# Loads in parts, input stages one at a time, and four attention ticks drawn into the last retention turn

## The chip, the cores and the metric

The kernel runs on one core of one Trainium2 chip. Its engines are TensorE (PE in the profile, with its weight loads as PEld), VectorE (DVE), ScalarE (ACT), GpSimd (POOL) and SyncE (SP), each with its own queue of instructions, worked off in order. The metric is the time of one execution on the device in microseconds (us), lower is better, given as a median of several runs.

## The reference

Two post-norm layers on `x` of shape (2, 1024, 128), all in float32:

```python
x = layernorm(x + retention(x))        # 8 heads of key width 64, value width 128: q, k rotated, decay mask,
                                       # group norm per head, gate silu(x Wg), output Wo
x = layernorm(x + mla_then_moe(x))     # x + mla(rmsnorm(x)): 16 heads of 8, keys and values from a latent
                                       # of 64, rotary, causal softmax; then x + moe(rmsnorm(x)), 4 experts,
                                       # hidden 512, each token goes through its best expert
x = layernorm(x + attention(x))        # 16 heads of 8, biases on q, k, v, softmax over all 1024 keys
                                       # (two corner scores set to -1e9)
x = layernorm(x + x @ ternary(weight)) # weight rounded to -1, 0, 1 times its mean size
```

## The kernel before

The 2048 tokens are two sequences (`b`) of 1024. Work goes by chunks of 128 tokens in the first part and by blocks of 512 tokens (`k` = 0, 1 in each sequence) in all later ones. Both parts are written inside `tc.manual_schedule()`: what the program emits first runs first on its engine.

**Retention turns.** A loop over `n_chunks` = 16 chunks holds one *turn* per chunk. Turn `n` finishes chunk `n - 1` and prepares the ones after it, in this order: `scores(n)` (PE `psc`, DVE `sm`, PE `pout` with the carried state), `keys_by_token` (PE `pk`, DVE `kd`), `sines(n + 1)` (POOL multiplies `swap` by the sine table), `rotated(n + 1)` (DVE adds `swap` into `qk`, POOL makes `qd`), `gated(n - 1)` and `affine` (PE `pt`, ACT `og`), `weighted` (PE `pout`), `carry` (PE `pst`, POOL `old`, DVE `state`), the DVE product `og * sg`, `group_norm(n)` (ACT `sq`, DVE `ss`, POOL `rstd`), `rotary(n + 2)` (PE `pr`, ACT `plain`, and four DMAs on SP's queue that copy `plain` into `swap` with its halves exchanged), `cosines(n + 2)`, `gate(n + 1)` (PE `pg`), `layer_norm` of a block that is complete, `aside(n, 0)`, `normal(n)` (DVE `on`), `output(n - 1)` (PE `py` with `r_wo`, DVE residual and statistics), `values(n + 1)` (PE `pv`), `aside(n, 1)` and `transpose_x(n + 3)` (PE `xT_ps`). `swap` for chunk 2, called swap(2) below, is thus issued in turn 0 and read by POOL at the start of turn 1.

**Late loads.** `load_late()` runs once ahead of turn 0 and issues 28 DMAs on SP: the rest of the rotary table `r_cs`, `r_wo`, then 13 weight slices, then 4 broadcasts of `mcs`, 8 small bias loads and `rowb`.

**Work drawn into the turns.** `aside(n, where)` looks up `plan[(n, where)]` and advances a generator by so many stages. The generators are `pad` (`padding(0)`: POOL clears `qT`, `v_aug`; ACT sets `kT`) and `ins[k]` (`mla_inputs(0, k, True)`), which makes queries, keys and values of block `k` of sequence 0. Its stages are `sq`; `ss`, `rstd`, `xn`; `xn_ps`, `xnT`; `pl`, `plat`; `stats` with the rotated queries (PE `mpr` twice, DVE `mrope` twice, DVE `dense`, four DMAs of `spread`); `apply`; `lat_ps`, `latT`; `mpv` with the rotated keys (again `mpr`, `mrope`, `dense`, `spread`). It needs block `k` after its `layer_norm`: block 0 is ready from turn 5 on, block 1 from turn 9.

**Banks.** The turns use PSUM pools `rps` (two buffers of two banks: `rwide`), `rpo` (two banks: `rbank`) and `racc` (two banks: `pout`). After the loop `rp.close()` frees all of them, and `ring_of` hands out eight banks in turn to all later work; the ring's pool waits for everything that used the freed memory. SBUF pools `late`, `work` and `jobs` likewise lie on memory that retention used.

**Attention ticks.** `chain_tick(t)` issues, for four heads, the scores of item `t` with their row maxima on DVE (`sc`, `spare` or `parts`), the transposed scores of item `t - AHEAD` with the exponentials on ACT (`sct`, `es`; `AHEAD` = 11), a causal cut on POOL (`bar`), and the products of item `t - 12` (PE `acc`, ACT `part`, POOL `oT`). Ticks 0 to 15 serve sequence 0, block 0; a step is 4 ticks there and 8 in block 1. `side_work(t)` runs ahead of tick `t` from tick 3 on and advances two lanes of `Job`s in order of their lists: the light lane is `padding(1)`, `setup()` (loads 2 MB of expert weights, makes the ternary weight), `mla_inputs(1, 0)`, `mla_inputs(1, 1)` and later ones; the heavy lane's experts begin at tick 30. A job not yet due at its tick holds up those behind it in its lane; a stage that yields 0 is followed by the next stage in the same tick.

After turn 15 the program before emits: `gated(15)`, `affine`, tick 0, the product `og * sg`, the last stage of `ins[1]`, tick 1, `output(15)`, tick 2, `layer_norm`, and then ticks 3 onwards with side work.

Of the kernel before, what the change touches and what calls it, by code (L numbers as in the profile page):

```python
# [14 lines left out]
P = 128  # L15
# [45 lines left out]
def block_kernel(  # L61
# [96 lines left out]
    def slot(name):  # L158
        return banks[0](name)

    def ring_of(pool):
        turn = [0]

        def bank(name):

            turn[0] += 1
            return pool.tile([P, BT], F32, tag=f"b{turn[0] % 8}", name=name)

        return bank

# [79 lines left out]
    def mla_inputs(b, k, alone=False):  # L250
        got = {}
        yield from rmsnorm_T(x1[b][k], col("norm1"), got)
        xnT = got["xnT"]

        def rotary_dense(dst, w, ws, src, tag):
            tt = scratch("mrope", "mrope", (P, 2, BT))
            table = mcs.rearrange("p (a t) -> p a t", a=2)[:, :, block_of(k)]
            for i, name in enumerate((w, ws)):
                pr = slot("mpr")
                mm(pr, name, src)  # L260
                if alone:
                    nc.vector.tensor_tensor(tt[:, i, :], pr, table[:, i, :], ALU.mult)
# [6 lines left out]
            engine.tensor_tensor(dense, tt[:, 0, :], tt[:, 1, :], ALU.add)  # L269
            spread(dst, k, dense)  # L270

        pl = by_tile(xnT, mw["wdkv"], "pl")
        plat = scratch("plat", "plat", (P, NC, 64))
        nc.scalar.copy(flat(plat), pl[:, : NC * 64])
        yield 1
        mv, r = stats(tiles(plat))
        rotary_dense(qT[b], mw["wq"], mw["wqs"], xnT, "sq")
        yield 2
        apply(tiles(plat), tiles(plat), mv, r)
        yield 1  # L280
        tp = slot("lat_ps")
# [3 lines left out]
        nc.scalar.activation(  # L285
            latT, tp[:64, :], AF.Identity, bias=col("ln_b", 0, 64), scale=col("ln_g", 0, 64)
        )
        yield 1
        pv = by_tile(latT, mk["wuv"], "mpv")
        nc.scalar.copy(  # L290
            v_heads(b)[:, k * NC : (k + 1) * NC, :, :HD],
            pv.rearrange("p (c h d) -> p c h d", c=NC, d=HD),
        )
        rotary_dense(kT[b], mk["wuk"], mk["wuks"], latT, "xn")
        yield 1

# [179 lines left out]


    with ExitStack() as rc:
        rp = ExitStack()
        rps = rp.enter_context(tc.tile_pool(name="rps", bufs=2, space=PSUM))  # L480
        rpo = rp.enter_context(tc.tile_pool(name="rpo", bufs=2, space=PSUM))
        racc = rp.enter_context(tc.tile_pool(name="racc", bufs=1, space=PSUM))
        rconst = rc.enter_context(tc.tile_pool(name="rconst", bufs=1))
        two = rc.enter_context(tc.tile_pool(name="r2", bufs=2))

# [31 lines left out]
        pads, padded = qT[0].rearrange("p g t -> p (g t)"), [0]  # L517

        def load_late():
            nc.sync.dma_start(out=cs[:, :, 2 * P :], in_=cs_in[:, :, 2 * P :])  # L520
            load_w("wo", nc.sync)
            for got, src, pack, n_rows, prefix in (
                (mw, m_w, M_W, P, "m"), (mk, m_k, M_K, 64, "mk"), (lw, l_w, L_W, P, "l")
            ):
                for name, (at, n) in pack.items():
                    if name not in ("w1", "w2"):
                        if n == NH * HW:
                            got[name] = pads[:n_rows, padded[0] : padded[0] + n]
                            padded[0] += n
                        else:  # L530
                            got[name] = const.tile([n_rows, n], F32, name=f"{prefix}_{name}")
                        nc.sync.dma_start(out=got[name], in_=src[:, at : at + n])
            for j in range(GH):
                nc.sync.dma_start(
                    out=mcs[dense_rows(j), :],
# [8 lines left out]
            nc.sync.dma_start(out=rowb, in_=rows.partition_broadcast(P))  # L544

        def dense_weights():

# [239 lines left out]
        def layer_norm(m, r):  # L787
# [22 lines left out]
        with tc.manual_schedule():  # L810
# [11 lines left out]
            for n in range(n_chunks):  # L822
                nxt, before = n + 1 < n_chunks, n > 0
# [4 lines left out]
                if nxt:  # L828
                    sines(n + 1)
                    rotated(n + 1)  # L830
# [11 lines left out]
                if nxt:  # L842
                    gate(n + 1)
                if block:
                    layer_norm(*block)
                    block = None
# [1 line left out]
                normal(n, r)  # L848
                if before:
                    block = output(n - 1, og)  # L850
                if nxt:
                    values(n + 1)
                aside(n, 1)
                if n + 3 < n_chunks:
                    transpose_x(n + 3)
                if n == 2:
                    dense_weights()

        rp.close()
# [36 lines left out]
    pools["work"] = ctx.enter_context(tc.tile_pool(name="work", bufs=2))  # L896
    jobs_sb = scratch_of[0] = ctx.enter_context(tc.tile_pool(name="jobs", bufs=1))

    def project(src, w, name, got, tag):

# [158 lines left out]
    class Job:  # L1059
# [179 lines left out]
```

## Time and profile before

| what | value |
|---|---|
| median of 3 runs | 1206.19 us (1205.71 to 1208.68) |
| the profiled execution's own time | 1211.32 us |
| its span, first to last instruction | 1209.6 us |
| mean granted clock of TensorE | 0.962 |
| busy: PE, PEld, DVE, ACT, POOL | 1112.6, 608.0, 830.1, 711.2, 479.0 us |
| start of turns 0, 1, 2 (first `psc`) | 21.4, 33.3, 54.8 us |
| start of turn 15 | 245.8 us |
| start of tick 4 on DVE, of tick 12 on DVE | 285.0, 308.8 us |

All durations below are from this one profiled execution, whose time is 5.1 us above the median. A busy share over the whole span mixes the retention turns (to about 280 us) with the attention ticks; a part of the change is read in the stretch where it lies. In a timeline line the first two numbers are start and duration, x is the count of instructions merged into it, and the bracket is the idle time of the engine before it with what ended that wait.

### The profile page before, as it was taken

To read this page: it belongs to the slowest core of one execution; us is meant where nothing else is said; L and a number is where in the kernel's file an instruction comes from. 1 tells how busy PE (TensorE), PEld (TensorE's weight loads), DVE (VectorE), ACT (ScalarE), POOL (GpSimd) and SP (SyncE) were. 2 spreads that over 40 slices of the span, in tenths; PEclk is the share of its full clock that TensorE was granted. 3 is DMA by queue.
4 is the path that set the end of the run, shared out by engine and by line. 5 is a ranking of instruction groups with operands and counts; after the bars stand their busy time and mean duration, and the time that the engine had idled before them with its cause. 6 is when DMAs were issued, how large, how long until landed. Compare 5 with 4: busy or idle time off the path is not lost.

```text
span 1209.6 us, 22194 instructions
## 1 busy us (share of the span) xinstructions
PE 1112.6 (92%) x8554; PEld 608.0 (50%) x8554; DVE 830.1 (69%) x1822; ACT 711.2 (59%) x1439; POOL 479.0 (40%) x491
## 2 busy tenths in 40 slices
PE   6899999988989999999999999999989989998993
PEld 5688778855444545455544454444433333333321
DVE  3467677657666666776666668667788878888822
ACT  2355544431656555654565547556768877886892
POOL 4365544513544433443434334333233333333342
PEclk9899999975889999999999999999999999999996
DMA  8211112102000000010000001000100000000000
GB/s 256 72 37 45 40 41 44 36 9 80 19 10 10 1 1 2 4 20 1 1 15 6 2 3 19 2 1 1 19 10 2 2 1 10 1 2 9 2 1 9
DMA packets 14841, 25.57 MB, mean 21 GB/s; under 512 B 2960, under 2 KB 8400, under 8 KB 14352
## 3 DMA queue, kind: packets, MB, share of 16 engines
q1 hardware_dynamic: 14080, 22.30, 7.6%
q8 instruction: 67, 1.10, 0.4%
q0 software_dynamic: 224, 1.05, 0.2%
q10 hardware_dynamic: 432, 0.81, 0.2%
q14 instruction: 38, 0.31, 0.1%
HBM read 10.13 MB, written 1.05 MB: 9 GB/s over the span
## 4 chain that ended last, share of the span: by engine, by line
PE 72%; DVE 15%; POOL 5%; issue 3%; ACT 2%; DMA 1%; SPq 0%; POOLq 0%; DVEq 0%; ACTq 0%
PE sc L82 16%; PE acc L82 15%; PE sct L82 12%; PE pmoe L82 5%; PE ph L82 5%; DVE parts L350 4%; DVE spare L345 2%; PE py L82 2%; PE pv L82 2%; PE pr L82 2%; PE pout L707 1%; PE pg L82 1%; ACT es L394 1%; PE o_ps L186 1%; PE psc L82 1%
## 5 line engine op out<-in xcount | busy, mean ns | idle before, releaser
L394 ACT ACTIVATE es<-sct 128x512 f32<-128x512 f32 (+3 forms) x896 | 427.4, 560 | 213.4 <-PE sct L82 160.9
L350 DVE TENSOR_REDUCE parts<-sc 128x1 f32<-128x512 f32 x640 | 397.4, 683 | 94.5 <-PE sct L82 67.0
L82 PE MATMUL sc<-kT,qT 32*128 32x512 f32 (+3 forms) x1792 | 427.1, 587 | 0.9 <-DVE parts L345 0.9
L82 PE MATMUL sct<-qT,kT 32*128 32x512 f32 (+3 forms) x1792 | 411.7, 577 | 1.4 <-DMA qT<-m_rows 1.1
L420 POOL TENSOR_TENSOR oT<-oT,part 128x512 f32<-128x512 f32 (+3 forms) x192 | 217.1, 1131 | 399.0 <-ACT part L419 395.0
L82 PE MATMUL acc<-es,v_aug 128*32 128x512 f32 (+3 forms) x1792 | 222.8, 561 | 40.0 <-DVE parts L350 28.4
L82 PEld LDWEIGHTS sc<-kT,qT 32*128 32x128 f32 x1792 | 169.9, 190 | 141.1 <-DVE parts L350 74.3
L82 PEld LDWEIGHTS sct<-qT,kT 32*128 32x128 f32 x1792 | 179.2, 184 | 45.0 <-issue 22.4
L345 DVE CUSTOM_DVE_ANT_0 spare<-sc,causal 128x512 f32<-128x512 f32 (+3 forms) x256 | 125.6, 490 | 55.5 <-PE sc L82 21.3
L82 PEld LDWEIGHTS acc<-es,v_aug 128*32 128x32 f32 x1792 | 37.9, 108 | 197.1 <-DVE parts L350 112.5
L419 ACT COPY part<-acc 128x512 f32<-128x512 f32 (+3 forms) x192 | 105.9, 552 | 42.6 <-PE acc L82 33.0
L402 POOL TENSOR_SCALAR_AFFINE_SELECT es<-es 128x512 f32<-128x512 f32 x64 | 40.6, 635 | 101.6 <-ACT es L394 101.6
L764 ACT ACTIVATE og<-pt,cols_sb 128x128 f32<-128x128 f32 x128 | 46.3, 467 | 37.5 <-PE pt L756 37.5
L82 PEld LDWEIGHTS pmoe<-m_w,hT 128*128 128x128 f32 x512 | 59.6, 192 | 15.9 <-DVE parts L350 8.8
L82 PE MATMUL pmoe<-m_w,hT 128*128 128x128 f32 x512 | 65.0, 280 | 0.4
L82 PE MATMUL ph<-xnT,m_w 128*128 128x512 f32 x128 | 62.4, 610 | 0.0
L118 POOL TENSOR_TENSOR rstd<-rstd,nhalf 128x4 f32<-128x4 f32 (+1 forms) x44 | 54.6, 1242 | 3.6
L638 POOL TENSOR_TENSOR swap<-swap,r_cs 128x1024 f32<-128x1024 f32 x16 | 38.7, 2419 | 26.4 <-DMA swap<-plain 26.4
L943 DVE TENSOR_SCALAR hT<-ph,cols_sb 128x512 f32<-128x512 f32 x32 | 24.0, 751 | 34.5 <-PE ph L82 34.5
L82 PE MATMUL py<-r_wo,og 128*128 128x128 f32 x256 | 37.0, 305 | 11.2 <-issue 5.4
L955 DVE SCALAR_TENSOR_TENSOR moe_acc<-pmoe,oh,moe_acc 128x128 f32<-128x128 f32 x64 | 22.5, 351 | 35.2 <-PE pmoe L82 34.8
L661 ACT COPY v<-pv 128x1024 f32<-128x1024 f32 x16 | 16.2, 1012 | 51.6 <-PE pv L82 51.6
(177 smaller groups left out, 1198.6 us busy)
## 6 DMA issues: line engine op xcount, KB each, us to landing
swap<-plain SPq DMA_DIRECT2D x64, 128.0 KB
qT<-dense SPq DMA_DIRECT2D x32, 64.0 KB
kT<-dense SPq DMA_DIRECT2D x32, 64.0 KB
m_w<-in_m_w SPq DMA_DIRECT2D x2, 1024.0 KB
x<-in_x SPq DMA_DIRECT2D x4, 256.0 KB
mcs<-in_m_const SPq DMA_DIRECT2D x4, 256.0 KB
out<-ob SPq DMA_DIRECT2D x4, 256.0 KB
r_rest<-in_r_const POOLq DMA_DIRECT2D x1, 774.0 KB, 7.9
```

The lines of the kernel that those rows point to most:

```text
L82: nc.tensor.matmul(o, lhsT, rhs, start=start, stop=stop)
L118: nc.gpsimd.tensor_tensor(r, r, nhalf[:, :n], ALU.pow)
L345: nc.vector.tensor_tensor_reduce(out=spare[:, :n], in0=sc[:, :n], in1=causal[:, BT - n :], scale=1.0, scalar=-3.0e38, op0=ALU.add, op1=ALU ...
L350: nc.vector.tensor_reduce(part, sc[:, :n], AX.X, ALU.max)
L394: nc.scalar.activation(es[n_item][:, j, :n], sct[:, :n], AF.Exp, scale=scale)
L402: nc.gpsimd.affine_select(out=d, in_=d, pattern=[[0, GH], [1, P]], compare_op=ALU.is_ge, fill=0.0, base=0, channel_multiplier=-1,)
L419: nc.scalar.copy(part[:, lo:], acc[:, lo:])
L420: nc.gpsimd.tensor_tensor(sums[i][:, lo:], sums[i][:, lo:], part[:, lo:], ALU.add)
L638: nc.gpsimd.tensor_tensor(swap[n], swap[n], table(n, 1), ALU.mult)
L764: nc.scalar.activation(og[:, a, g, :], pt[a][:, g, :], AF.Identity, bias=col("gn_b", h), scale=col("gn_w", h))
L943: nc.vector.tensor_scalar(hT[:, f, :], ph, bias, 0.0, ALU.add, ALU.max)
L955: nc.vector.scalar_tensor_tensor(acc[:, c, :], py[:, :P], oh[:, c, e : e + 1], acc[:, c, :], ALU.mult, ALU.add)
```

## The change

`load_late` becomes a generator in three parts: `r_cs` and `r_wo` are issued ahead of turn 0 as before; the 13 weight slices after `rotary(2)` in turn 0; the 13 DMAs of `mcs`, biases and `rowb` after `rotary(3)` in turn 1. `mla_inputs` gets two more places to pause, and `plan` now takes nearly every place once, one stage at a time, from (5, 1) on; block 1's stages all lie in turns 11 to 15. The last turn is written out by itself: its PSUM accumulators `racc` get a pool on the other side that closes only after `normal(15)`, the ring gets six banks first and two later, ticks 0 to 3 are placed among the last chunk's steps, and the ring and the SBUF pools `late`, `work`, `jobs` wait tile by tile. `setup()` may start from tick 12 only.

```diff
-    def ring_of(pool):
+    def ring_of(pools):
...
+            at = turn[0] % 8
             turn[0] += 1
-            return pool.tile([P, BT], F32, tag=f"b{turn[0] % 8}", name=name)
+            return pools[at // 6].tile([P, BT], F32, tag=f"b{at}", name=name)
...
         mv, r = stats(tiles(plat))
+        yield 0
         rotary_dense(qT[b], mw["wq"], mw["wqs"], xnT, "sq")
...
+        yield 0
         rotary_dense(kT[b], mk["wuk"], mk["wuks"], latT, "xn")
...
-        rp = ExitStack()
+        rs, rp = ExitStack(), ExitStack()
+        racc = rs.enter_context(tc.tile_pool(name="racc", bufs=1, space=PSUM, side="right"))
...
-        racc = rp.enter_context(tc.tile_pool(name="racc", bufs=1, space=PSUM))
...
             load_w("wo", nc.sync)
+            yield
...
                         nc.sync.dma_start(out=got[name], in_=src[:, at : at + n])
+            yield
...
             nc.sync.dma_start(out=rowb, in_=rows.partition_broadcast(P))
+            yield
...
-            (3, 1): (pad, 1), (4, 1): (pad, 1), (5, 1): (pad, 1), (6, 1): (pad, 3),
-            (7, 0): (ins[0], 2), (7, 1): (ins[0], 1), (8, 0): (ins[0], 1), (8, 1): (ins[0], 1),
-            (9, 0): (ins[0], 1), (9, 1): (ins[0], 1), (10, 0): (ins[0], 2),
-            (12, 0): (ins[1], 2), (13, 1): (ins[1], 1), (14, 0): (ins[1], 1),
-            (15, 0): (ins[1], 1), (15, 1): (ins[1], 2), (16, 0): (ins[1], 2),
+            (3, 1): (pad, 1), (4, 0): (pad, 1), (4, 1): (pad, 1), (5, 0): (pad, 3),
+            (5, 1): (ins[0], 1), (6, 0): (ins[0], 1), (7, 0): (ins[0], 1), (7, 1): (ins[0], 1),
+            (8, 0): (ins[0], 1), (8, 1): (ins[0], 1), (9, 0): (ins[0], 1), (9, 1): (ins[0], 1),
+            (10, 0): (ins[0], 1), (10, 1): (ins[0], 2),
+            (11, 0): (ins[1], 1), (11, 1): (ins[1], 1), (12, 0): (ins[1], 1), (12, 1): (ins[1], 1),
+            (13, 0): (ins[1], 1), (13, 1): (ins[1], 1), (14, 0): (ins[1], 1), (14, 1): (ins[1], 1),
+            (15, 0): (ins[1], 1), (15, 1): (ins[1], 2),
...
-            load_late()
+            late_loads = load_late()
+            next(late_loads)
...
+                next(late_loads, None)
+                gate(n + 1)
...
+            n = n_chunks - 1
+            sm = scores(n)
+            pt, og = gated(n - 1)
+            affine(n - 1, pt, og, range(RH))
+            weighted(n, sm)
+            nc.vector.tensor_tensor(og, og, sg[n - 1], ALU.mult)
+            r = group_norm(n)
+            aside(n, 0)
+            output(n - 1, og)
...
-        banks[0] = ring_of(ctx.enter_context(tc.tile_pool(name="ring", bufs=1, space=PSUM)))
-
+        ring.append(ctx.enter_context(
+            tc.tile_pool(name="ring", bufs=1, space=PSUM, reuse_waits="tile")
+        ))
+        banks[0] = ring_of(ring)
         with tc.manual_schedule():
-            n = n_chunks - 1
+            chain_tick(0)
+            normal(n, r)
+            rs.close()
+            ring.append(ctx.enter_context(tc.tile_pool(
+                name="ring2", bufs=1, space=PSUM, side="right", reuse_waits="tile"
+            )))
+            aside(n, 1)
+            chain_tick(1)
             pt, og = gated(n)
             affine(n, pt, og, range(RH))
-            chain_tick(0)
+            chain_tick(2)
             nc.vector.tensor_tensor(og, og, sg[n], ALU.mult)
-            aside(n_chunks, 0)
-            chain_tick(1)
             block = output(n, og)
-            chain_tick(2)
+            chain_tick(3)
             layer_norm(*block)
...
-    late = ctx.enter_context(tc.tile_pool(name="late", bufs=1))
+    late = ctx.enter_context(tc.tile_pool(name="late", bufs=1, reuse_waits="tile"))
...
-        Job(0, ends(0, 0, 0), setup()),
+        Job(12, ends(0, 0, 0), setup()),
...
-        for tick in range(3, last_tick):
+        for tick in range(4, last_tick):
```

More of the change, by code (lines that the diff above doesn't have):

```diff
@@ L819, in block_kernel @@
             rotated(0)
-            load_late()
+            late_loads = load_late()
+            next(late_loads)
             block = None
-            for n in range(n_chunks):
-                nxt, before = n + 1 < n_chunks, n > 0
+            for n in range(n_chunks - 1):
+                before = n > 0
                 keeps = not opens(n + 1)
@@ L827, in block_kernel @@
                     kd = keys_by_token(n)
-                if nxt:
-                    sines(n + 1)
-                    rotated(n + 1)
+                sines(n + 1)
+                rotated(n + 1)
                 if before:
@@ L841, in block_kernel @@
                     cosines(n + 2, rotary(n + 2))
-                if nxt:
-                    gate(n + 1)
+                next(late_loads, None)
+                gate(n + 1)
                 if block:
@@ L850, in block_kernel @@
                     block = output(n - 1, og)
-                if nxt:
-                    values(n + 1)
+                values(n + 1)
                 aside(n, 1)
@@ L857, in block_kernel @@
                     dense_weights()
+            n = n_chunks - 1
[7 more added lines that the diff above has]
+            output(n - 1, og)
+        ring = []
         rp.close()
-        banks[0] = ring_of(ctx.enter_context(tc.tile_pool(name="ring", bufs=1, space=PSUM)))
+        ring.append(ctx.enter_context(
+            tc.tile_pool(name="ring", bufs=1, space=PSUM, reuse_waits="tile")
+        ))
+        banks[0] = ring_of(ring)
         with tc.manual_schedule():
-            n = n_chunks - 1
+            chain_tick(0)
[6 more added lines that the diff above has]
+            chain_tick(1)
             pt, og = gated(n)
             affine(n, pt, og, range(RH))
-            chain_tick(0)
+            chain_tick(2)
             nc.vector.tensor_tensor(og, og, sg[n], ALU.mult)
-            aside(n_chunks, 0)
-            chain_tick(1)
             block = output(n, og)
-            chain_tick(2)
+            chain_tick(3)
             layer_norm(*block)
     x2 = x1
-    late = ctx.enter_context(tc.tile_pool(name="late", bufs=1))
+    late = ctx.enter_context(tc.tile_pool(name="late", bufs=1, reuse_waits="tile"))
     for i, name in enumerate(("w1", "w2")):
@@ L895, in block_kernel @@
     )
-    pools["work"] = ctx.enter_context(tc.tile_pool(name="work", bufs=2))
-    jobs_sb = scratch_of[0] = ctx.enter_context(tc.tile_pool(name="jobs", bufs=1))
+    pools["work"] = ctx.enter_context(tc.tile_pool(name="work", bufs=2, reuse_waits="tile"))
+    jobs_sb = scratch_of[0] = ctx.enter_context(tc.tile_pool(name="jobs", bufs=1, reuse_waits="tile"))
     def project(src, w, name, got, tag):
```

## The prediction

> **What bounds the kernel now.** The row of 40 slices comes first: PE is at 9 tenths nearly everywhere, so the long run of attention ticks is PE's and nothing in this change touches its work. Time can be won only where PE's digit drops: slices 1 and 2, and those around 240 to 310 us.
>
> ```profile
> PE   6899999988989999999999999999989989998993
> PEclk9899999975889999999999999999999999999996
> ```
>
> The chain of waits and the timeline of 10 to 62 us show the first hole. Turn 1 runs from `psc` at 33.4 to `psc` at 54.8, turns 2 and 3 take 13.64 us each.
>
> ```profile
> 43.44 5.37 issue
> 48.81 3.75 PE py L82 x16
> ...
> 64.85 1.79 PE py L82 x16
> ```
>
> ```profile
> 15.64 0.58 SPq L520 DMA_DIRECT2D r_cs<-in_r_const  x1
> 34.24 0.44 SPq L544 DMA_DIRECT2D rowb<-in_rows  x1
> 34.80 10.33 SPq L625 DMA_DIRECT2D swap<-plain  x8
> 40.91 2.35 POOL L638 TENSOR_TENSOR swap<-swap,r_cs 128x1024 f32<-128x1024 f32 x1 [10.06 <-DMA swap<-plain]
> 48.81 3.75 PE L82 MATMUL py<-r_wo,og 128*128 128x128 f32 x16 [5.39 <-issue]
> ```
>
> The chain calls it "issue", but the cause is readable: SP issues the late loads from 15.64 to 34.68, `plain` for chunk 2 is ready at 30.0, its swap DMAs go out at 34.80, POOL gets them at 40.91, and `sines`, `rotated`, `qd`, `old`, `state`, `og` follow one another until `py` may start. After the pause `py` takes 3.75 us instead of 1.79.
>
> The second hole is the handover from turn 15 to the ticks (timelines of PE and DVE, 232 to 312 us).
>
> ```profile
> 256.29 3.76 PE L82 MATMUL py<-r_wo,og 128*128 128x128 f32 x16 [3.93 <-DVE mrope L262]
> 263.13 1.97 PE L756 MATMUL pt<-ident,on 128*128 128x128 f32 x8 [0.86 <-ACT latT L285]
> 274.06 3.78 PE L82 MATMUL py<-r_wo,og 128*128 128x128 f32 x16
> ```
>
> ```profile
> 267.26 0.69 DVE L345 CUSTOM_DVE_ANT_0 spare<-sc,causal 128x512 f32<-128x512 f32 x1 [5.47 <-PE sc L82]
> 284.98 0.68 DVE L345 CUSTOM_DVE_ANT_0 spare<-sc,causal 128x512 f32<-128x512 f32 x1
> 308.78 0.68 DVE L345 CUSTOM_DVE_ANT_0 spare<-sc,causal 128x512 f32<-128x512 f32 x1
> ```
>
> The three DVE lines are the first row maximum of ticks 0, 4 and 12: tick 4 begins 39.2 us after turn 15 (245.8), and DVE stands idle 5.47 us before tick 0. From tick 4 to 12 there are only scores, and DVE sets the pace (first row below: 19.0 of 23.8 us busy, PE at clock 0.56, so slow, not short of time). From tick 12 on PE does.
>
> ```profile
> core 0: us, PE busy (x) PEld busy (x) DVE busy (x) ACT busy (x) POOL busy (x), PEclk, DMA share, GB/s
> 285.00:308.80 23.80, 22.59 (x88) 13.06 (x88) 19.00 (x83) 4.31 (x8) 5.33 (x9) 0.56 0.01 3
> 308.80:368.80 60.00, 53.62 (x412) 27.72 (x411) 38.35 (x115) 36.12 (x89) 33.26 (x38) 0.91 0.07 14
> 368.80:382.20 13.40, 12.36 (x105) 5.38 (x102) 10.57 (x27) 9.59 (x21) 4.49 (x6) 1.00 0.10 21
> ```
>
> The last two rows are ticks 12 to 25, with `mla_inputs` of sequence 1 among them, and ticks 26 to 29 without: 4.29 against 3.35 us a tick.
>
> **The change, part by part.** *Loads in three parts.* SP has 2 DMAs ahead of turn 0 instead of 28. swap(2) goes out at 30.0 instead of 34.8; four issues take 2.4 us, and in an undisturbed turn the data is there 1.8 us later (issued 119.80 to 122.2, used at 123.99). POOL starts at about 34.3, ends 36.7; `rotated` 37.9, `qd` 39.2, `old` 40.3, `state` 41.1, `og` 42.3. `pg` ends at 43.4, so `py` no longer waits, and turn 1 falls from 21.4 to the 13.64 of its neighbours: **-7.8 us**. Moved past: part two (13 DMAs, 8.4 us of SP: 16.8 to 25.2 before) follows swap(2), from 32.4 to 41, and `plain` for chunk 3 is ready at 42.7: free by then. Part three (13 DMAs, 9.5 us) follows swap(3), 45.1 to 54.6, then the load of `x`; swap(4) wants SP at about 56. Both fit with 1 to 2 us to spare, and a turn can bear `sines` some 1.7 us late (0.7 us until `rotated` is due, 1.0 between `og` and `py`). `r_wo` landed by about 21.7, when SP's wait for it ended.
>
> *Turns 5 to 14.* Turn lengths are differences of `psc` starts; a turn without extras is 13.64, turn 7 (no `pk`, `pst`, as a new sequence follows) 12.2. Turn 7 took 16.0: POOL made `xn` while PE waited 2.80 us, and the next `psc` took 2.08 instead of 1.09. With `sq` and `xn` done in turns 5 and 6 it costs only `xn_ps` and `pl`: 13.65, **-2.35**. Turn 8 (`mpr` 1.7, no `pl`) 15.4 for 16.55, **-1.15**. Turn 9: DVE's `layer_norm`, `apply`, `normal` still hold up `xT_ps`, but start earlier: 15.0 for 15.96, **-1.0**. Turns 10, 11: **-0.4**. Turn 12 gets worse: `ss` at (11, 1) lies on DVE behind `output`, so POOL's `rstd` and `xn` end near 206.5 on the old time scale and `sines(13)`, queued behind them, starts 3.2 us late; `og`, `py` and `pv` follow 1.3 us late, and `xn_ps` and `pl` add 1.5: **+2.85**. In turn 13 `stats` (1.3) and `layer_norm` (1.1) both lie ahead of `normal`, whose `output` must free a bank for the second `mpr`: **+0.7**. Turn 14 **-0.2**. Sum: **-1.5**. The four DMAs of each `spread` (2.9 us of SP at 159.51) still lie between two swap groups some 14 us apart, and delay none. The earlier `pad` stages are memsets of 1.0 us at places where POOL is idle.
>
> Here a rule of the Trainium skill speaks against the change. The row: `dense` on DVE takes 0.69 us alone, but
>
> ```profile
> 157.19 2.29 DVE L269 TENSOR_TENSOR dense<-mrope 128x512 f32<-128x512 f32 x1
> ```
>
> while POOL's `sines` ran from 156.58 to 158.94. "SBUF — State Buffer" (section on the two separate sides) says that a DVE instruction with two SBUF inputs and a GpSimd instruction that reads SBUF exclude each other for a whole instruction. The plan puts three `dense` at places (n, 1), just where the next `sines` starts. By the rule each may lose up to 2 us, and `sm` behind it: +4 to +6. In my order of queues POOL's `sines` is nearly done when `dense` comes (its `swap` lands before the `mpr`), so I charge 0.5, inside the turn lengths above.
>
> *Turn 15 to tick 4.* Counted from `psc` of turn 15: `pout` is done at 4.8 as before, `mpv` takes 1.1, and `py` waits only for `og` at 7.3 instead of 10.5. `py` 2.0 (after a pause of 1.4 us it was 2.02 at 228.6), tick 0's scores to 10.3, its maxima (3.4) to 13.8, `normal` to 15.0, `mrope` and `dense` to 17.1. Two of tick 1's banks wait for `normal` (new wait: `sc` and `pt` are queued behind it, PE idle 2.9). Maxima of tick 1 (2.85) to 20.0, of tick 2 (2.3) to 22.4, `og` to 23.6, `py` 3.75 to 27.4, residual 1.0, tick 3's maxima 1.8, `layer_norm` 2.0: about 32.6 against 39.2: **-6.6**. The clock is the choice here. "TensorE: Matmul & The Clock Gate" (part 1) has half rate after an idle window of about 3.4 us, and full rate only after as long a busy stretch. By the rule the 2.9 us pause may leave PE warm and `py` at 1.8, -8.6 in all; the row (3.93 idle, then 3.76) says cold, and `py` comes after a second pause of about 4 us, so I take cold.
>
> *Ticks 4 to 34.* With `setup` held to tick 12, the light lane is empty after `padding(1)`: DVE loses the ternary (1.4), `ss` (0.7) and `stats` (1.5) from its pace between ticks 4 and 12: **-3.4** of 23.8. They come back later: `mla_inputs(1, 0)` and `(1, 1)` now lie wholly in ticks 14 to 34. Before, 14 ticks took 60.0 for 14 x 3.35 = 46.9; less 2.5 for starting the exponentials, 1.6 of these jobs cost 10.6, so 6.6 each. Another 0.4 costs 2.6, the ternary 0.5: **+3.1**. Bounds: zero if PE's gaps hide it, +6 if POOL's `mrope` and `dense` (2.36 + 1.27) hold up the causal cut each time. The 2 MB of expert weights took from 278.3 to 286 and would hold one `m_rows` DMA about 7 us, seven ticks ahead of its use: zero. The additional yields of 0 cost nothing in a lane. Waits tile by tile remove the wait of POOL's `v_aug` clearing for retention's end, hidden either way; after tick 34 the order is the same and PE-bound, so an earlier start is kept.
>
> Sum: -7.8 - 1.5 - 6.6 - 3.4 + 3.1 = **-16.2**. Profiled execution 1211.3 to 1195.1; it was 5.1 above the median of 1206.19, so **1190**.
>
> **The rivals.** *More comes (chance 0.20):* `py` stays warm (-2), turn 12 hides its late `sines` (-1.3), the moved jobs fill PE's gaps (-3.1): 1184. For it: PE is idle 6.4 of 60 us in ticks 12 to 25. *Half is given back (0.20):* `dense` collides as the rule says (+5) and the moved jobs cost +6 instead of +3.1: 1198; for it speaks POOL at 33 of 60 us there. *Slower (0.06):* the delayed jobs. If ticks 12 to 34 (308.8 to 398.8, 3.9 each) rise to 4.8, because every POOL pair stalls `acc` and experts join from tick 30, that is +20 beyond the sum, 1210. It decides from 4.75 a tick; against it, ticks 12 to 25, the densest with such jobs, had 4.29. *Nothing (0.07):* swap(3) and swap(4), now behind a part of the loads each, come over 5 us late and cost turns 2 and 3 what turn 1 gains: about 1204.
>
> **How the numbers follow.** The likeliest case has 0.47. A measurement of this kernel can tell some 0.3% (3.6 us) from no change. Faster takes all but the last two cases: 0.87. The range reaches from 1180, a little past the second case, to 1200, past the third.
>
> **What would show it.** Turn 1 at 13.6 and POOL's wait for swap(2) gone; turn 7 near 13.7, turns 12 and 13 at 16 to 17; turn 15 near 236; tick 4 about 33 us after it; ticks 4 to 12 in 20.4 us. I am wrong if the swaps of chunks 3 or 4 are waited for, or if ticks 12 to 34 take over 95 us.

## The result, and the profile after

| what | before | after |
|---|---|---|
| median | 1206.61 us (4 runs, 1205.71 to 1208.68) | 1194.08 us (4 runs, 1191.54 to 1195.23) |
| ratio, with 95% interval | | 0.9884 (0.9863 to 0.9904) |
| profiled execution, own time and span | 1211.32, 1209.6 us | 1191.54, 1189.8 us |
| mean granted clock of TensorE | 0.962 | 0.975 |
| start of turns 0, 1, 2 | 21.4, 33.3, 54.8 us | 20.4, 32.4, 46.0 us |
| start of turn 15 | 245.8 us | 235.4 us |
| start of tick 4, tick 12, tick 35 on DVE | 285.0, 308.8, 398.8 us | 268.9, 290.6, 378.4 us |

The time was forecast at 1190 and came out at 1194. From tick 35 to the end of the span both kernels take the same (810.8 and 811.4 us), so all that happened lies ahead of it.

The two rows of the 40 slices, as shown of before: in slice 2, where turn 1 lies, PE's digit is now 9 instead of 8, and so is that of the granted clock. The dip of the clock in slices 9 and 10 is the handover and the ticks behind it; before, it reached from slice 9 to slice 12 (7, 5, 8, 8).

```profile
PE   6999999979889999999999999999989989998993
PEclk9999999986999999999999999999999999999996
```

The chain of waits from 38 to 48 us (start, duration, what) is now PE's work without a break: `py` takes 1.79 us, and there is no "issue" of 5.37 us ahead of it.

```profile
38.69 1.98 PE pr L82 x16
40.67 1.79 PE pg L82 x16
42.46 1.79 PE py L82 x16
44.25 1.72 PE pv L82 x4
45.97 0.11 PE xT_ps L612
46.08 1.09 PE psc L82 x16
```

The timelines of SP and POOL show why. swap(2) is issued as soon as `plain` is there, at 29.06, and POOL has it at 33.47 after 3.59 us of waiting instead of 10.06. Part two of the loads follows, and swap(3) goes out at 41.75, 3.3 us after the last of them ended.

```profile
29.06 2.42 SPq L632 DMA_DIRECT2D swap<-plain  x4
31.52 1.08 SPq L537 DMA_DIRECT2D qT<-in_m_w  x2
...
37.99 0.44 SPq L537 DMA_DIRECT2D l_wt<-in_l_w  x1
41.75 2.45 SPq L632 DMA_DIRECT2D swap<-plain  x4
```

```profile
33.47 2.37 POOL L645 TENSOR_TENSOR swap<-swap,r_cs 128x1024 f32<-128x1024 f32 x1 [3.59 <-DMA swap<-plain]
```

The handover from turn 15 to the ticks, on PE and on DVE. `py` of chunk 14 follows turn 15's start by 7.4 us instead of 10.5; `py` of chunk 15 starts at 261.11, behind three score matmuls of tick 4 (the line `x6`) that the program's PE order puts ahead of it. The program text emits them behind `py`, so on PE the order of the text is not strictly kept here, unlike what the description of the kernel says. DVE's three lines are the first row maximum of ticks 0, 4 and 12.

```profile
242.76 3.19 PE L82 MATMUL py<-r_wo,og 128*128 128x128 f32 x16 [1.44 <-DVE og L871]
251.92 0.93 PE L82 MATMUL sc<-kT,qT 32*128 32x384 f32 x8 [2.53 <-DVE on L748]
257.60 3.58 PE L82 MATMUL sc<-kT,qT 32*128 32x512 f32 x6 [1.87 <-DVE parts L348]
261.11 3.38 PE L82 MATMUL py<-r_wo,og 128*128 128x128 f32 x16
```

```profile
247.51 0.69 DVE L348 CUSTOM_DVE_ANT_0 spare<-sc,causal 128x512 f32<-128x512 f32 x1 [0.68 <-PE sc L82]
268.92 0.67 DVE L348 CUSTOM_DVE_ANT_0 spare<-sc,causal 128x512 f32<-128x512 f32 x1
290.59 0.69 DVE L348 CUSTOM_DVE_ANT_0 spare<-sc,causal 128x512 f32<-128x512 f32 x1 [1.13 <-PE sc L82]
```

Busy time by stretch, ticks 4 to 12 and the 60 us behind them (columns: stretch, length, busy time of PE, PEld, DVE, ACT, POOL with counts, granted clock, DMA share, GB/s). DVE's busy time between ticks 4 and 12 fell from 19.00 to 16.40 us, yet PE is still at clock 0.50, and is busy for 21.05 of 21.70 us.

```profile
268.90:290.60 21.70, 21.05 (x75) 14.50 (x74) 16.40 (x70) 3.90 (x6) 2.70 (x5) 0.50 0.26 98
290.60:350.60 60.00, 53.94 (x464) 27.90 (x458) 44.30 (x131) 38.62 (x98) 32.83 (x42) 0.99 0.05 11
```

### The profile page after: what moved, and what is told of

Same layout as the page of the kernel before. It is cut to its first block, busy times and chain, and to the rows that moved or that the text cites. A ratio compares the mean times of both kernels' runs of the same rounds, so it can differ in the third digit from the quotient of the medians.

```text
span 1189.8 us, 22189 instructions
## 1 busy us (share of the span) xinstructions
PE 1102.6 (93%) x8554; PEld 604.3 (51%) x8554; DVE 825.9 (69%) x1822; ACT 710.4 (60%) x1439; POOL 479.8 (40%) x491
## 4 chain that ended last, share of the span: by engine, by line
PE 72%; DVE 17%; POOL 4%; issue 3%; ACT 2%; DMA 1%; SPq 0%; POOLq 0%; DVEq 0%; ACTq 0%
PE sc L82 17%; PE acc L82 15%; PE sct L82 12%; PE pmoe L82 5%; PE ph L82 5%; DVE parts L353 5%; DVE spare L348 2%; PE py L82 2%; PE pv L82 2%; PE pr L82 2%; PE pout L714 1%; PE o_ps L187 1%; PE pg L82 1%; DVE x L205 1%; ACT es L397 1%
## 5 line engine op out<-in xcount | busy, mean ns | idle before, releaser
L82 PEld LDWEIGHTS ph<-xnT,m_w 128*128 128x128 f32 x128 | 21.7, 189 | 31.0 <-issue 11.0
```

Source lines behind the costliest of these rows:

```text
L82: nc.tensor.matmul(o, lhsT, rhs, start=start, stop=stop)
```

## The experiments

Each kernel was timed in five rounds against the kernel before, whose median was 1207.9 to 1208.0 us in all three groups of runs. "Turn 15 to tick 4" is the time from the first `psc` of turn 15 to the first row maximum of tick 4 on DVE; before has 39.2 us in its profiled execution, the changed kernel 33.6.

**e1_loads_only: the kernel before, with the late loads in three parts.**

```diff
             load_w("wo", nc.sync)
+            yield
...
-            load_late()
+            late_loads = load_late()
+            next(late_loads)
...
+                next(late_loads, None)
                 if nxt:
                     gate(n + 1)
```

> The kernel before with the loads in three parts and nothing else. If the stall of turn 1 is all of this part (my step of -7.8 us), turn 1 falls from 21.4 to 13.6 us, all later turns keep their lengths, and the kernel is 7 to 9 us faster than before. If the parts only move the queueing, a later turn (2 or 3) grows by what turn 1 gains, and the time is within 2 us of before.

Measured: 1202.26 us (1197.67 to 1206.35), ratio 0.9951 (0.9932 to 0.9970), which is 5.9 us less (3.6 to 8.2). In its trace turn 1 takes 13.6 us and turns 2 to 4 keep their 13.6: there the part does by itself what it does in the change. The median fell by less than the 7 to 9 us expected; the interval reaches into that range, and why the median shows less was not found.

This run showed a second thing. From turn 15 on its program has the order of before, but turn 15 to tick 4 took 36.6 us, not 39.2. The timeline of PE has `py` of chunk 15 and the rotated keys at full clock:

```profile
259.85 1.02 PE L82 MATMUL mpr<-latT,m_dense_wuks 64*128 64x512 f32 x2
260.80 0.93 PE L82 MATMUL sc<-kT,qT 32*128 32x384 f32 x8
262.64 2.05 PE L82 MATMUL py<-r_wo,og 128*128 128x128 f32 x16 [0.91 <-DVE og L872]
```

In the profiled execution of before the same three groups took 1.91, 1.66 and 3.78 us. So 2.6 us of that execution's handover belonged to its clock, not to the kernel's order. Ticks 16 to 24 are the same case: 32.2 us there, with a clock of 0.70 from 350 to 359 us, and 30.0 us here, at 1.00. (This execution is the fastest of e1_loads_only's eleven, 4.6 us below their median, so it shows what the clock can take, not what a median execution of before has.)

**e2_plan_only: the kernel before, with the new plan and the two further places to pause.** Loads in one piece, the old handover (ticks 0 to 2), `setup` not held.

```diff
         mv, r = stats(tiles(plat))
+        yield 0
...
-            (15, 0): (ins[1], 1), (15, 1): (ins[1], 2), (16, 0): (ins[1], 2),
+            (15, 0): (ins[1], 1), (15, 1): (ins[1], 2),
```

(and the other lines of `plan` as in the change)

> The kernel before with the new plan of stages and the two pauses, loads and handover as before. My steps: turns 5 to 14 shorter by 1.5 us in sum, with turn 12 up by 2.9 and turn 7 down by 2.4; the handover, which no longer has the last stage of block 1 between ticks 0 and 1, shorter by 2 to 4 us. Together 3 to 6 us faster. The rival, that the stages only matter together with the ticks placed in the last turn, says within 1.5 us of before.

Measured: 1202.01 us (1197.80 to 1204.60), ratio 0.9951 (0.9933 to 0.9969). All turns but turn 1 (21.2 us) are as in the changed kernel, and turn 15 to tick 4 takes 30.8 us: the old order of ticks, and less than the changed kernel's 33.6. The first score row of turn 15 and the first row maximum of tick 4, from PE's and DVE's timelines, here and then in e5_old_handover (below), where 32.3 us lie between them:

```profile
243.62 1.16 PE L82 MATMUL psc<-qk 64*128 64x128 f32 x16
274.41 0.68 DVE L347 CUSTOM_DVE_ANT_0 spare<-sc,causal 128x512 f32<-128x512 f32 x1
```

```profile
239.47 1.16 PE L82 MATMUL psc<-qk 64*128 64x128 f32 x16
271.78 0.68 DVE L348 CUSTOM_DVE_ANT_0 spare<-sc,causal 128x512 f32<-128x512 f32 x1
```

Against the 36.6 us of e1_loads_only, what shortened the handover is thus the plan, and not the four ticks drawn into it: of block 1 only `mpv` and the rotated keys are left behind turn 15's start, where before the rotated queries and `lat_ps` came there too.

**e3_no_hold and e4_after_again: the changed kernel with `setup` due from tick 0, and the changed kernel once more beside it.**

```diff
-        Job(12, ends(0, 0, 0), setup()),
+        Job(0, ends(0, 0, 0), setup()),
```

> The changed kernel, but setup() may start at once (tick 4) instead of at tick 12. My sum gave -3.4 and +3.1 for the hold, so the same time as the changed kernel within 2 us. The trace of the changed kernel shows ticks 4 to 35 taking 109.5 us against 113.8 before: if the hold is what makes them shorter, this run is about 4 us slower than the changed kernel, with ticks 12 to 16 back at 17 to 18 us instead of 12.

> The changed kernel on the same chip as the three others, to set them against. 11 to 15 us faster than before; with the granted clock of each run beside its span, runs that differ in time should differ by about 1 us for each 0.001 of clock.

Measured: without the hold 1198.04 us (1196.27 to 1199.25), ratio 0.9923 (0.9904 to 0.9943); with it 1194.32 (1191.66 to 1197.02), ratio 0.9895 (0.9874 to 0.9916). The hold is worth about 3.7 us, and the traces say the same: ticks 4 to 35 take 113.9 us without and 110.1 with it. The second of the two expectations of e3_no_hold came true, the first (within 2 us) did not. Time and mean clock of the six runs of e4_after_again mostly go together, from 1191.66 us at 0.975 to 1197.02 at 0.968, but the run with the highest clock, 0.977, took 1193.66, so 1 us for each 0.001 is no fixed rate. By stretch, first the kernel without the hold, ticks 8 to 12 and 12 to 16, then the one with it:

```profile
283.90:298.70 14.80, 14.55 (x60) 8.00 (x64) 9.31 (x42) 5.90 (x10) 4.47 (x7) 0.56 0.00 2
298.70:315.90 17.20, 14.86 (x117) 7.43 (x114) 10.26 (x38) 10.20 (x25) 8.32 (x10) 0.90 0.08 17
```

```profile
281.30:293.00 11.70, 11.70 (x47) 8.56 (x48) 8.38 (x36) 3.91 (x6) 0.48 (x1) 0.50 0.47 181
293.00:305.60 12.60, 11.70 (x104) 5.42 (x101) 9.83 (x41) 7.74 (x21) 6.54 (x10) 0.88 0.01 2
```

Unheld, `setup` and `mla_inputs(1, 0)` cost 1.6 us in ticks 4 to 8, 3.1 in the next four and 4.6 in the four behind tick 12, 9.3 in all. Held, these jobs run at the full clock from tick 16 on and bring back 5.5 (1.1 in ticks 16 to 24, and 45.7 us for 41.3 in ticks 24 to 35). Part of the gain repairs a loss: in the old order, without a hold, ticks 4 to 35 took 111.0 us (e1_loads_only). Why the same jobs cost more behind the new handover (ticks 8 to 12 take 14.8 us in e3_no_hold, 12.1 in e1_loads_only) was not tested.

**e5_old_handover: the changed kernel, with before's order after turn 15** (`normal` and the last stage ahead of tick 0, ticks 0 to 2, one ring of eight banks, side work from tick 3).

```diff
+            normal(n, r)
             output(n - 1, og)
+            aside(n, 1)
...
-            chain_tick(0)
-            normal(n, r)
-            rs.close()
...
-            chain_tick(1)
             pt, og = gated(n)
             affine(n, pt, og, range(RH))
-            chain_tick(2)
+            chain_tick(0)
             nc.vector.tensor_tensor(og, og, sg[n], ALU.mult)
+            chain_tick(1)
             block = output(n, og)
-            chain_tick(3)
+            chain_tick(2)
             layer_norm(*block)
```

> The changed kernel with the handover of before: normal, output and the last input stage inside turn 15, one ring of eight banks after the loop, ticks 0 to 2 around the last chunk's steps; loads, plan, hold and the waits of the SBUF pools as changed. If the placing of the four ticks is worth my -6.6 us (the step of turn 15 to tick 4), this run is 4 to 7 us slower than the changed kernel. The trace of the plan-only run speaks for the rival: with the new plan and the old handover tick 4 came 30.8 us after turn 15, against 33.5 in the changed kernel, so this run is 1 to 3 us faster, and the gain of that step was the plan's.

Measured: 1194.43 us (1190.25 to 1199.00), ratio 0.9882 (0.9857 to 0.9906); turn 15 to tick 4 in 32.3 us, and 32.3 in the changed kernel run again (e4_after_again). Neither of the expected differences came. Drawing four ticks in, and freeing the banks in two steps for it, shows no gain and no loss: six executions with the changed order (this kernel twice, and e3, e7, e8, e9) took 31.6 to 34.4 us from turn 15 to tick 4.

**e6_og_first: the changed kernel, with the last chunk's gate product ahead of tick 2.**

```diff
             affine(n, pt, og, range(RH))
+            nc.vector.tensor_tensor(og, og, sg[n], ALU.mult)
             chain_tick(2)
-            nc.vector.tensor_tensor(og, og, sg[n], ALU.mult)
             block = output(n, og)
```

> The changed kernel with one line moved: the product og times sg of the last chunk stands ahead of tick 2 instead of behind it on VectorE. If the late py (waiting for og behind 2.4 us of maxima, VectorE then idle 4.3 us for py) is what makes the new handover no shorter than the old, tick 4 comes 2 to 3 us earlier after turn 15 (30.5 to 31.5 us) and the kernel is 2 to 3 us faster than the changed one. If TensorE at half clock is the limit there, it is within 1 us of it.

Measured: 1191.12 us (1190.32 to 1193.14), ratio 0.9857 (0.9839 to 0.9874). Turn 15 to tick 4 falls to 30.5 us, below all six executions with the changed order (31.6 to 34.4). DVE's timeline, changed kernel first: there the product `og` waits behind tick 2's maxima, and DVE then has nothing to do for 4.33 us until `py` is done; with the product first the wait is 1.81. On PE, `py` now also comes ahead of tick 4's three score matmuls, so the run removes both delays at once and does not tell them apart. The interval of the times overlaps that of the changed kernel; it is the traces that show the gain, somewhere between 1 and 4 us, as each is a single execution and the clock differs between them.

```profile
258.97 1.22 DVE L896 TENSOR_TENSOR og<-og,sg 128x1024 f32<-128x1024 f32 x1
264.52 0.29 DVE L788 TENSOR_TENSOR x<-py,x 128x128 f32<-128x128 f32 x1 [4.33 <-PE py L82]
```

```profile
257.60 1.23 DVE L895 TENSOR_TENSOR og<-og,sg 128x1024 f32<-128x1024 f32 x1
262.70 0.29 DVE L788 TENSOR_TENSOR x<-py,x 128x128 f32<-128x128 f32 x1 [1.81 <-PE py L82]
```

**e7_pool_waits: the changed kernel, with the pools `late`, `work` and `jobs` waiting as a whole.**

```diff
-    late = ctx.enter_context(tc.tile_pool(name="late", bufs=1, reuse_waits="tile"))
+    late = ctx.enter_context(tc.tile_pool(name="late", bufs=1))
```

(and the same for `work` and `jobs`)

> The changed kernel with the SBUF pools late, work and jobs waiting as a whole again (the ring still tile by tile). My text gave these waits nothing: the same time within 1 us, with the clearing of v_aug on GpSimd back behind the end of retention. The rival: the clearing of kT on ScalarE and the first exponentials wait too, and ticks 4 to 16 get 2 us longer.

Measured: 1195.62 us (1193.39 to 1199.07), ratio 0.9890 (0.9871 to 0.9908), no different from the changed kernel. The rival is out as well: ticks 4 to 16 take 33.8 us, for 34.3 in e4_after_again. POOL's clearing of `v_aug` again waits for the end of retention, 19 us, and nobody waits for it:

```profile
271.13 1.21 POOL L233 MEMSET v_aug<- 128x1336 f32 x1 [19.16 <-DVE x L788]
```

**e8_sq_early: the changed kernel, with the first two stages of block 1 one place earlier**, so that POOL's `rstd` and `xn` come ahead of the sines of turn 12.

```diff
-            (10, 0): (ins[0], 1), (10, 1): (ins[0], 2),
-            (11, 0): (ins[1], 1), (11, 1): (ins[1], 1), (12, 0): (ins[1], 1), (12, 1): (ins[1], 1),
+            (10, 0): (ins[0], 1), (10, 1): (both, 3),
+            (11, 0): (ins[1], 1), (12, 0): (ins[1], 1), (12, 1): (ins[1], 1),
```

(`both` takes two stages of `ins[0]` and then one of `ins[1]`)

> The changed kernel with the first two stages of block 1 half a turn and a turn earlier: sq at (10, 1), ss and xn at (11, 0), nothing at (11, 1). If the late sines on GpSimd behind xn is what lengthens turn 12 (py 0.81 us late behind og), turn 12 falls from 16.1 to about 15.2 us and the kernel gains 1 us. If the wait moves to turn 11 instead, turn 11 grows from 13.6 by as much, and the time is the same.

Measured: 1193.24 us (1189.08 to 1193.56), ratio 0.9864 (0.9844 to 0.9883). By the runs alone that is not told apart from the changed kernel; the trace is clear. Turns 11, 12 and 13 take 13.6, 14.9 and 15.8 us instead of 13.6, 16.1 and 16.5. POOL's sines start 1.9 us earlier, although turn 12 itself begins 0.7 us later, and PE no longer waits for `og` ahead of `py`. Changed kernel first, POOL and then PE; then the same of this one:

```profile
192.90 2.36 POOL L645 TENSOR_TENSOR swap<-swap,r_cs 128x1024 f32<-128x1024 f32 x1
200.94 2.02 PE L82 MATMUL py<-r_wo,og 128*128 128x128 f32 x16 [0.81 <-DVE og L847]
```

```profile
191.01 2.36 POOL L645 TENSOR_TENSOR swap<-swap,r_cs 128x1024 f32<-128x1024 f32 x1
200.65 1.95 PE L82 MATMUL py<-r_wo,og 128*128 128x128 f32 x16
```

**e9_center_early: the changed kernel, with the centering of the value weights ahead of the first cosines.** The traces so far had shown turn 0 starting at one of two times: 20.4 to 21.4 us in six of them, 24.1 to 25.2 in four. The edit takes away what the two cases differ in.

```diff
+            center()
             for n in range(2):
                 cosines(n, rotary(n))
-            center()
```

> The changed kernel with the subtraction of center() emitted ahead of the first rotary cosines instead of behind them. In the executions so far the subtraction on VectorE and the first swap of GpSimd start within 0.2 us of each other and the one that comes second takes some 3.3 us longer; turn 0 then starts at 20.4 to 21.2 us or at 24 to 25.2 us. Theory (the two engines hold each other up, and the order is a race): with the subtraction out of the way early, the race is gone, turn 0 starts at the same time in each execution, between 18 and 20.5 us, and the time falls by 1 to 4 us against the 1194 us of the changed kernel, with less spread between its runs. Rival (the start is set by a landing weight, and the subtraction waits for it ahead of the cosines): turn 0 stays at 21 us or later and the time within 1 us of 1194.

Measured: 1191.00 us (1187.82 to 1191.86), ratio 0.9860 (0.9834 to 0.9885), turn 0 at 18.6 us. The timelines of DVE and POOL, in the changed kernel, in its second execution (e4_after_again), and here:

```profile
14.00 1.23 DVE L583 TENSOR_TENSOR r_wv<-r_wv,r_mean 128x1024 f32<-128x1024 f32 x1
14.16 3.25 POOL L645 TENSOR_TENSOR swap<-swap,r_cs 128x1024 f32<-128x1024 f32 x1 [10.15 <-DMA swap<-plain]
```

```profile
14.50 2.34 POOL L645 TENSOR_TENSOR swap<-swap,r_cs 128x1024 f32<-128x1024 f32 x1 [10.49 <-DMA swap<-plain]
14.54 3.38 DVE L583 TENSOR_TENSOR r_wv<-r_wv,r_mean 128x1024 f32<-128x1024 f32 x1
```

```profile
10.53 1.23 DVE L583 TENSOR_TENSOR r_wv<-r_wv,r_mean 128x1024 f32<-128x1024 f32 x1
14.81 2.35 POOL L645 TENSOR_TENSOR swap<-swap,r_cs 128x1024 f32<-128x1024 f32 x1 [10.79 <-DMA swap<-plain]
```

Whichever of the two engines starts second, by as little as 0.04 us, is held until the other's instruction is done. Early centering parts them: what turn 0 then waits for is `swap`, whose landing varies too (turn 0 starts at 18.2 to 18.6 us in three executions with this edit, and at 20.6 in e12_all_hold16). The runs still spread over 4.0 us (3.7 and 5.4 in the two groups of the changed kernel), so the smaller spread that the theory expected was not seen, and the interval overlaps the changed kernel's.

**e10_og_sq_center: the three edits e6, e8 and e9 together.**

> The three edits together: the last chunk's gate product ahead of the maxima of tick 2, the late sine of turn 11 two places earlier, and the subtraction of center() ahead of the cosines. If the three places are independent, their gains add: 3.2 us between turn 15 and tick 4, 1.3 us in turns 12 and 13, and 1 to 4 us at the start, so 1186 to 1189 us against 1194. Rival (what is gained ahead of the experts is given back where TensorE's clock is halved or the jobs collide): 1190 us or more.

Measured: 1186.36 us (1184.19 to 1187.93), ratio 0.9819 (0.9792 to 0.9846): the best version of all, and its interval lies clear of the changed kernel's. Against e4_after_again its span is 8.7 us shorter. By stretch: turn 0 starts 5.5 us earlier (1.8 against the other execution of the changed kernel, which had the early start), the turns take 1.8 less, turn 15 to tick 4 1.5 less (30.8 for 32.3), ticks 4 to 35 the same 110.1. The gains of the three edits add up as far as the intervals can tell, and nothing is given back where the clock is halved.

**e11_all_keys_late: e10, with the last stage of block 1 (the rotated keys) behind the last chunk's projection steps.**

```diff
-            aside(n, 1)
             chain_tick(1)
             pt, og = gated(n)
             affine(n, pt, og, range(RH))
+            aside(n, 1)
             nc.vector.tensor_tensor(og, og, sg[n], ALU.mult)
```

> As the three edits together, and with the tick 1 part of the last chunk's handover moved behind its projection. Theory (the chunk's projection is waited for by VectorE, and less work ahead of it brings it earlier): tick 4 starts 1 to 2 us sooner after turn 15. Rival (VectorE's work before tick 4 is the same in sum, only its order changes): tick 4 within 0.5 us of the run with the three edits.

Measured: 1190.34 us (1187.73 to 1191.58), ratio 0.9851 (0.9823 to 0.9878). Both the theory and the rival fell: turn 15 to tick 4 grew from 30.8 to 34.7 us. The keys' matmuls had filled the time in which PE waits for `normal`. Without them PE pauses 3.81 us, and they follow later at half the clock, 2.07 and 1.91 us for 1.12 and 1.02, with DVE waiting for each:

```profile
254.09 2.07 PE L82 MATMUL mpr<-latT,m_dense_wuk 64*128 64x512 f32 x2
256.20 0.69 DVE L263 TENSOR_TENSOR mrope<-mpr,mcs 128x512 f32<-128x512 f32 x1 [2.63 <-PE mpr L82]
```

The other 2.4 us of the longer span (1189.9 for 1183.7) come from its start, where the program is the same; they are told in the last section.

**e12_all_hold16: e10, with `setup` held to tick 16.**

> As the three edits together, and with the setup job held to tick 16 instead of tick 12. Theory (a held job costs less the later it runs, as tick 12 against tick 0 brought 3.7 us): ticks 12 to 16 shrink from 12 to about 9.5 us and 0.5 to 1.5 us of it stays. Rival (the jobs behind it are then late for the experts): what is gained comes back after tick 30, and the time is 0 to 5 us above that of the three edits.

Measured: 1188.13 us (1186.88 to 1189.06), ratio 0.9834 (0.9809 to 0.9860). Ticks 12 to 24 take 37.4 us instead of 42.5, ticks 24 to 35 51.1 instead of 45.7, and from tick 35 to the end it is 813.4 us instead of 811.1. By the runs alone the two are not told apart, their intervals overlap; in the traces the rival came true, and a little more than what was gained comes back. The job with the rotated keys of sequence 1's second block, done by tick 32 in e10, now reaches into tick 36 and lies there among the experts' matmuls; that tick takes 7.5 us for 4.6, with DVE idle 2.89 us for its next scores. PE's timeline in that tick:

```profile
379.19 1.98 PE L82 MATMUL ph<-xnT,m_w 128*128 128x512 f32 x4
381.11 1.16 PE L82 MATMUL mpv<-mk_wuv,latT 64*128 64x128 f32 x8
382.10 1.02 PE L82 MATMUL mpr<-latT,m_dense_wuk 64*128 64x512 f32 x2
```

Ahead of tick 12 the two executions come out even: `swap` landed 2.0 us later at the start, and the handover, whose program is the same, took 28.9 us for 30.8.

## Why the prediction was right, point by point

| step | predicted | profiled pair |
|---|---|---|
| start to turn 0 | 0 | -1.0 |
| turn 1 | -7.8 | -7.8 |
| turns 5 to 14 | -1.5 | -1.7 |
| turn 15 to tick 4 | -6.6 | -5.7 |
| ticks 4 to 12 | -3.4 | -2.1 |
| ticks 12 to 35 | +3.1 | -2.2 |

- **Turn 1** was read right to a tenth, by the chain that e1_loads_only then showed alone: SP's queue delays swap(2), and POOL's sines delay all that follows. The loads cost nothing where they went; swap(3) and swap(4) left on time, so the rival in which nothing is gained is out.
- **Turns 5 to 14.** Turn 12 was forecast at 16.5 and took 16.1, for the reason given, as e8_sq_early shows. Single turns were off by up to 0.8 us (turn 14: 13.2, forecast 12.4), the sum by 0.2.
- **The shared-port rule** was charged at 0.5 us. It holds: two of the three `dense` on DVE that stand at places (n, 1) met POOL's `sines` and took 1.97 and 1.01 us, the third 0.69. That is 1.6 us in all, not 4 to 6. The first delay reached turn 9: `sm` began 2.7 us behind `psc` instead of 1.2, PE stood 0.41 us ahead of `pout`, and the turn took 15.6 us for the 15.0 forecast; what share of these 0.6 us is the collision's was not tested. Behind the second, `pout` came at its usual time.
- **Turn 15 to tick 4** has the right order of size and the wrong cause. The prediction counted it along the path through the newly placed ticks, and did not ask what the plan alone would bring; e5_old_handover shows no gain from the ticks' place, and e2_plan_only all of it from the plan. That the sum fits is in part luck. The path's length was forecast well (32.6 us, 33.6 and 32.3 measured). What it missed on that path is that three score matmuls of tick 4 stand ahead of `py` on PE, which began 0.9 us after `og` was done. That DVE has no work while `py` runs (4.33 us measured) it had in its sum as 3.75 us, but it did not ask for the order that e6_og_first tried, in which `og` goes ahead of tick 2's maxima and the wait is 1.81. The last `py` ran at half the clock, as chosen; `py` of chunk 14, taken at 2.0 us, was 3.19 in the profiled execution and 2.05 in the second.
- **The hold of `setup`** was sized at -0.3 us net, and is worth 3.7 (e3_no_hold against e4_after_again). The mis-sized terms are both prices of the moved jobs: -3.4 and +3.1 were forecast where these two runs show -9.3 and +5.5. Against the old order (111.0 us in e1_loads_only, 109.5 in the changed kernel) 1.5 us are left of it. The prediction knew only what DVE spends on a job between ticks 4 and 12, and took DVE to set the pace there. DVE's busy time fell by 2.6 us, the stretch by 2.1, to 21.7 us where 20.4 was forecast, and PE was then busy for 21.05 of it at a clock of 0.50. It had no row for what the jobs cost in ticks 8 to 16 by themselves, where TensorE's clock is 0.50 to 0.90 and the exponentials start. The feared case, over 4.75 us a tick from tick 12 to 34, was far off: 87.8 us for 23 ticks is 3.8.
- **Tile-by-tile waits** at zero: right (e7_pool_waits).
- **From the sum to the median** is where the forecast was weakest. The sum for the profiled execution was 1195.1, and 5.1 was taken off because that execution was 5.1 slower than the median. e1_loads_only shows two stretches in which it was slower with the same program: 2.6 us in the handover and 2.2 in ticks 16 to 24, both at a lower clock (0.56 against 0.77 in the last 30 and 28 us ahead of tick 4, and 0.92 against 1.00). The first of these the handover's step had already taken away, since it was set against 39.2 and not against 36.6. Without counting it twice the forecast would have been 1192.6, an estimate from these two executions, which would account for most of the 4 us by which it lay low. What a median execution of before has in the handover was not seen. Nor can the profiled pair decide this: its spans differ by 19.8 us, the medians by 12.5, since the profiled execution of before is slower than the four runs it is set against, and that of after is the fastest of its own four.
- **Luck in the total.** In the profiled pair, ticks 12 to 35 came out 5.3 us better than forecast, of which 2.2 are the clock of before, while the handover and ticks 4 to 12 brought 2.2 less than forecast. That 1190 came so near rests in part on such errors cancelling.

The parts add up as far as the intervals can tell: loads 5.9 us, plan 5.9, hold 3.7, ticks and waits none, 15.5 in all, against 14.0 (11.6 to 16.5) by the ratio of the changed kernel; the repaired loss above is counted in the hold's 3.7.

## What to carry to other kernels

Ask of each queue what stands in front of the one transfer that the next step waits for: bulk loads that nothing waited for cost 7.8 us of turn 1 here by keeping one `swap` waiting on SP's queue for 4.8 us. When a forecast is built on one profiled execution, look whether a stretch at a lower clock lies inside a part that the change touches; what is gained there should not be taken off a second time as an offset. And when work is moved away from a wait, ask whether it was what kept TensorE busy during that wait.

## What the runs showed of the hardware

**A race at the start between VectorE and GpSimd.** The centering on DVE, with two SBUF inputs in its last instruction, and POOL's first product on `swap`, which reads SBUF, start within 0.4 us of each other (not always 0.2, as the expectation of e9_center_early has it), and the second one waits out the first. The Trainium skill ("SBUF — State Buffer", section on the two separate sides) calls the shared port pair an exclusive lock for the whole instruction, and these rows agree with it: 1.23 us became 3.38, or 2.35 became 3.25. In the other three executions in which POOL came first, the instruction held was the small scaling ahead of the subtraction, 1.97 to 2.25 us for 0.17. The two outcomes are uneven. If DVE comes first, turn 0 starts at 20.4 to 21.4 us; if POOL does, `pv` waits for the late subtraction and turn 0 starts at 24.1 to 25.2. The changed kernel's two executions, 20.4 and 24.1, are one of each kind.

**Short pauses and the clock.** After the same pause of 1.4 us, `py` of chunk 14 took 3.19 us in the changed kernel, 2.05 in its second execution and 3.68 in e10_og_sq_center, with a granted clock of 0.61, 1.00 and 0.50 in the 2 us behind the pause. Of the twelve executions with that pause, six have 2.05 us and six 3.09 to 3.68. The pause is shorter than the idle window of about 3.4 us that the prediction cited from the Trainium skill ("TensorE: Matmul & The Clock Gate", part 1); here the measurement decides. In e11_all_keys_late a pause of 2.58 us ahead of `psc` in turn 0 (1.31 to 1.86 in e9, e10 and e12, at full clock) was followed by a clock of 0.50 from 20 to 26 us, and the turn took 2.8 us longer:

```profile
18.25 1.16 PE L82 MATMUL psc<-qk 64*128 64x128 f32 x16 [2.58 <-DVE qk L648]
20.73 3.78 PE L714 MATMUL pout<-v,sm 128*128 128x128 f32 x16 [0.71 <-DVE sm L682]
```

In e10 the same `pout` took 2.05 us. `pg` had ended at 15.7 us instead of 16.7, while `psc`, which waits for `swap`, began only 0.3 us sooner: that made the pause longer. That the longer pause is what lowered the clock rests on these four executions and was not tested by an edit.
